# A decoder layer with a mixture of experts: attention scores in single PSUM banks, up to four row groups per step, and a planner that shares places and paces its preparations

## The chip, the core and the metric

The kernel runs on one core of one Trainium2 chip. The metric is the device time of one execution in microseconds (us); times of several executions are given by their median.

## The reference

One decoder layer over 32 sequences of 128 tokens, D = 128 features, 16 heads of 8 features. In short:

```python
def attn(q_in, kv_in, w, causal):          # B=32, S=128, H=16, HD=8
    Q, K, V = (heads(a @ w_ + b_) for ...)  # (B, S, H, HD)
    s = einsum('bqhd,bkhd->bhqk', Q, K) / sqrt(8)
    if causal: s = where(tril, s, -inf)
    return einsum('bhqk,bkhd->bqhd', softmax(s), V).reshape(B, S, D) @ w.wo + w.bo

x = layernorm(x + attn(x, x, sa, causal=True))        # self-attention
x = layernorm(x + attn(x, ctx_1024, ca, causal=False)) # cross-attention
p = softmax(x @ router_w + router_b)                   # E = 8 experts
topw, topi = top_k(p, 2); topw = softmax(topw)
# each token: sum over its 2 experts of
#   topw * (gelu(x @ w1[e] + b1[e]) @ w2[e] + b2[e]),  FF = 512, exact gelu
x = layernorm(x + moe)
```

All inputs and the output are float32. The 4096 tokens go to two experts each, so 8192 rows of 128 features pass through the experts' layers.

## The kernel before

**A planner orders the work.** The class Timetable (L80 to L195) holds every step of the kernel as a Task: an engine, a planned duration, a function that emits the instructions, the tasks it depends on, a priority, and the buffers that it takes from rings or uses. Timetable.run plays the steps through: an engine takes, whenever it is free, the ready task of the best priority whose buffers are free, and the instructions are emitted in that order. A step that depends on another engine's may start HOP = 0.35 us after it. The planned durations are constants in the code; they set only the order, and the chip's own times can differ. Engines are PE (TensorE), DVE (VectorE), ACT (ScalarE), POOL (GpSimd) and SP (which only issues transfers here).

**PE's rule.** On PE, a step that is not a score step goes first. A score step may be paired with a "mate" of the other kind and the other half h of the heads; the function emit_scores (L198) then emits the instructions of both in turn, lane by lane.

**Attention.** pair_item (L516 to L862) handles a pair of sequences p, once for self-attention ("s") and once for cross-attention ("c"): 16 pairs, 32 items. Its steps: load of x or of the context by SP (L536); transposes (PE L547, copied out by ACT); projections to Q and K (PE L590 and L591; ACT L595 and L600 copy them into tile qk); projection to V (PE L614, copied by DVE L618 into one of three v tiles); masking by heads on POOL (L631): from qk it makes kb and qb, in which each 32-row group holds four heads, with one head's rows kept for each 128 columns.

The scores are computed twice. by_query (L651) has queries on partitions, into tile bq: for each of two row groups of 32 rows, a product of 32 x 128 with 32 x 512 in float32 and, for self-attention, four causal masks of 32 x 512 in bfloat16 (L659), which add a large negative number. DVE takes the maximum over the keys (L675, 128 x 1024 in one instruction), splits it into three bfloat16 parts (L688 to L691), PE transposes them (L697) and DVE copies them (L702). by_key (L716) has keys on partitions, into tile bk, again two row groups of 512 columns; then "less" (L723) subtracts the queries' maxima by products in bfloat16, and the causal masks are added (L731). ACT takes exp (L746, 128 x 1024) into a pr tile, and PE multiplies with v (L760). Each item has two sequences and two halves h of the heads, so four by_query and four by_key steps. Tiles bq and bk are two PSUM banks each, and there is one of each; four further banks m0 to m3 take all other PE results.

Then: uT copy on ACT (L773), transposes back (PE L781), division by the sums on DVE (L789 and L790), transposes again, output projection (PE L807), addition of the residual (DVE L812), layer norm (normalize, L864: statistics on DVE L872 and L874, the reciprocal root on POOL L880 and L881, the rest on DVE L818 or L832). After cross-attention the normed rows lie twice in xrow, each with a number that tells where its result goes (L841); POOL makes x2 for the residual (L850 and L853); and route (L897 to L1022, once for each pair) computes the router's logits, the two best experts, their weights, and each row's place in its expert's region, and POOL scatters the rows to a DRAM tensor rowsD with one indirect transfer per 128 rows (L1010).

**Start.** PE first runs 14 products on zeros (pidle). ACT's queue carries, in this order, the loads of the attention's weights (L261 to L270), the filling of rowsD with empty rows (L463 and L468: ten transfers of 1548 KB, one of 1032 KB, two of 64.5 KB), the packing of the experts' weights into a DRAM tensor wpack (L469, L471, L476), and the load of b1 (L474). PE's first transpose after pidle is that of b1, pb (L481), and its result goes on into wpack (L484). sa.constant and ca.constant (L426 to L432) fold bv and wo into bo.

**Experts.** PHASES splits the sequences into the first 24 and the last 8. table(f) (L1070) works out on DVE, from the counts of rows per expert, a list of blocks of 4, 2 or 1 times 128 rows of one expert each: for the first phase 5, 7 and 21 blocks, for the second 23 blocks of 128 rows, that is 78 times 128 rows. block() (L1144): SP reads the block's expert and first row into registers and fetches rows (tile xg) and the expert's packed weights (tile wt, 578 KB) (L1153 to L1167); PE transposes (L1174), DVE copies (L1180), PE multiplies with w1 (L1194), ACT takes gelu (L1207), PE multiplies with w2 (L1222), DVE adds b2 (L1232), POOL scatters the result rows to DRAM tensor resD (L1239). The first transposes of a block wait in the plan for the last exp of the attention. Rings: xg 4, wt 4, xgT 2, h 2, y 3. final() (L1251): SP loads both results of each token (fyl, L1264), DVE adds them with their weights (L1277, L1280), layer norm, POOL L1296 and L1297, store by SP (L1302); ring yl of 3.

Of the kernel before, what the change touches and what calls it, by code (L numbers as in the profile page):

```python
# [9 lines left out]
F32 = mybir.dt.float32  # L10
# [13 lines left out]
S2 = 2  # L24
RG = 4
# [6 lines left out]
WROW = 2 * FF + NC + P  # L32
NOWHERE = 1 << 20
# [46 lines left out]
class Timetable:  # L80
# [3 lines left out]
    HOP = 0.35  # L84

    def __init__(self):
        self.tasks = []
        self.rings = {}
        self.tile = {}

    def ring(self, name, bufs):
        self.rings[name] = list(bufs)

# [5 lines left out]
    def run(self):  # L99
# [16 lines left out]
        def can(t):  # L116
            need = {}
            for r, k in t.acq:
                if k not in held:
                    need[r] = need.get(r, 0) + 1  # L120
            return all(len(self.rings[r]) >= n for r, n in need.items())

        def start(t, now, dur):
            for r, k in t.acq:
                if k not in held:
                    held[k] = (r, self.rings[r].pop(0))
                    self.tile[k] = held[k][1]
            waiting[t.eng].remove(t)
            t.end = now + dur
            heapq.heappush(ending, (t.end + t.lat, t.n, t))  # L130
            heapq.heappush(events, (t.end, -1))

        def finish(t, now):
            for a in t.after:
# [6 lines left out]
            for k in {*t.uses, *(k for _, k in t.acq)}:  # L141
                users[k] -= 1
                if not users[k]:
                    r, b = held.pop(k)
                    self.rings[r].append(b)

        while events:
# [5 lines left out]
            for e in waiting:  # L153
                while free[e] <= now + 1e-9:
# [4 lines left out]
                    pick = ok[0]  # L159
                    mate = None  # L160
                    if e == "PE" and any(t.kind for t in ok):
                        for t in ok:
                            if t.kind is None:
                                pick = t
                                break
                            mate = next(
                                (
                                    m for m in ok
                                    if m.kind and m.kind[0] != t.kind[0] and m.kind[1] != t.kind[1]
                                ),  # L170
                                None,
                            )
                            if mate:
                                pick = t
                                break
                        else:
                            pick = ok[0]
                    if mate is None:
                        start(pick, now, pick.dur)
                        pick.emit(self.tile) if not pick.kind else emit_scores([pick.emit], self.tile)  # L180
                        free[e] = now + pick.dur
                    else:
                        dur = max(pick.dur, mate.dur)
                        start(pick, now, dur)
                        start(mate, now, dur)
                        emit_scores([pick.emit, mate.emit], self.tile)
                        free[e] = now + dur
# [3 lines left out]
        if done != len(self.tasks):  # L191
            for e, w in waiting.items():
                print(e, [(t.n, t.acq, t.kind) for t in w][:20])
            print({k: v[1] for k, v in held.items()})
            raise AssertionError  # L195


def emit_scores(parts, tiles):  # L198

    lanes = [lane for part in parts for lane in part(tiles)]  # L200
# [7 lines left out]
def kernel(  # L208
# [37 lines left out]
    assert sum(n for n, _ in PHASES) == B  # L246
# [5 lines left out]


    idle = const.tile([P, 512], BF16, name="idle")
    nc.vector.memset(idle, 0.0)
    pidle = psum.tile([P, 512], F32, tag="m0", name="pidle")
    for _ in range(14):
        nc.tensor.matmul(pidle, lhsT=idle[:, :P], rhs=idle, start=True, stop=True)


    def load(src, shape, name, eng=nc.scalar):  # L261
        t = const.tile(shape, F32, name=name)
        eng.dma_start(out=t, in_=src)
        return t

    def column(src, name):
        return load(src.rearrange("(p o) -> p o", o=1), [P, 1], name)

    def row(src, n, name):
        return load(src.rearrange("(o n) -> o n", o=1).broadcast_to([P, n]), [P, n], name)  # L270

    T = Timetable()
    DUR = dict(xin=3, xT=3, qk=3, kb=5, qb=6, v=3, pr=5, t3=4, nmT=3, uT=2, o=2, oT=2, xn=3, xr=3,
               xrow=4, x2T=2)
    SHAPE = dict(
        xin=([P, S2, P], F32), xT=([P, S2, P], F32), qk=([P, 2, S2, P], F32),
        kb=([P, 4, P], F32), qb=([P, 4, P], F32), pr=([P, 8, P], F32),
        nmT=([P, P], BF16), uT=([P, S2, 2, P], F32), o=([P, S2, P], F32), oT=([P, S2, P], F32),
        xn=([P, S2, P], F32), xr=([P, S2, P], F32), xrow=([P, S2, 2, ROW], F32),
        x2T=([P, S2, P], F32),  # L280
    )
    for name, n in DUR.items():
        T.ring(name, [f"{name}{i}" for i in range(n)])
    T.ring("bq", ["bq"])
    T.ring("bk", ["bk"])
    T.ring("open", ["open0", "open1"])
    T.ring("m", ["m0", "m1", "m2", "m3"])
    NF = 6
    SMALL = ("nm", "ri", "st", "mv", "rs", "rt")
    for name in SMALL:  # L290
        T.ring(name, [f"{name}{i}" for i in range(NF)])

    def tl(key, shape=None, dtype=F32, name=None):

        tag = T.tile[key]
        base = tag.rstrip("0123456789")
        if shape is None:
            shape, dtype = SHAPE[base]
        T.tile[key] = work.tile(shape, dtype, tag=tag, name=name or f"{key[0]}_{'_'.join(map(str, key[1:]))}")
# [15 lines left out]
    def bank(key, shape, dtype=F32):  # L315

        tag = T.tile[key]
        n = 1024 if tag in ("bq", "bk") else 512
        flat = psum.tile([P, n], F32, tag=tag, name=f"{key[0]}_{'_'.join(map(str, key[1:]))}")
# [3 lines left out]

    ident = const.tile([P, P], F32, name="ident")
    make_identity(nc, ident)
    ident16 = const.tile([P, P], BF16, name="ident16")
    nc.vector.tensor_copy(ident16, ident)


    id32f = const.tile([P, RG, 32], F32, name="id32f")  # L330
    nc.vector.tensor_copy(id32f, ident.rearrange("p (g i) -> p g i", g=RG))
    id32 = const.tile([P, 32], BF16, name="id32")
    with nc.allow_low_precision("sums of zeros and a one"):
        nc.vector.tensor_reduce(id32, id32f.rearrange("p g i -> p i g"), AX.X, ALU.add)

    cauq = const.tile([P, 4, P], BF16, name="cauq")
    cauk = const.tile([P, 4, P], BF16, name="cauk")
    for t, s in ((cauq, 1), (cauk, -1)):  # L340
        nc.gpsimd.memset(t, 0.0)
        for g in range(RG):
            r = t[32 * g : 32 * g + 32]
            nc.gpsimd.affine_select(
# [1021 lines left out]
```

## Time and profile before

| | |
|---|---|
| three executions | 1180.70, 1196.39, 1190.12 us; median 1190.12 |
| the profiled execution: time | 1188.61 us |
| its span (first to last instruction) | 1186.8 us |
| mean granted TensorE clock in it | 0.712 of full |
| busy: PE, DVE, POOL, ACT | 950.9, 508.4, 409.8, 297.3 us |
| PE busy, 93 to 893 us (attention) | 749.7 of 800 us |
| PE busy, 893 to 1047 us (experts, first phase) | 121.6 of 154 us |
| first transpose of x; end of the last exp | 89.0 us; 887.4 us |

How to read the views. The page's slices cut the span into 40 equal parts of 29.7 us; a digit is the busy share in tenths, PEclk the granted clock in tenths, DMA the mean share of the 16 DMA engines. The table by stage gives for each engine the busy time and the number of instructions, then the granted clock, the DMA share and GB/s. A timeline line has start, duration, engine, line, operation, destination and sources, the tile on the array (rows*columns), and the size of the moving operand; instructions that belong together are put on one line with a count, and what an engine waited for stands in brackets. In the view of waits, an engine's line is followed by what it waited for, the total in us, the number of waits and the longest. PE's records give streaming time from a model of its pipeline, so the distance from one start to the next is the safer measure of a step.

### The profile page before, as it was taken

What the parts mean: (1) busy time and instruction counts of PE and PEld (TensorE: products, weight loads), DVE (VectorE), ACT (ScalarE), POOL (GpSimd) and SP (SyncE); (2) the same over time, 40 slices, a digit from 0 to 9 for tenths busy, and PEclk for the clock granted to TensorE, in tenths of its full rate; (3) what the DMA queues carried; (4) which work ended last, traced back from release to release, by engine and by line L of the source; (5) the groups of instructions that cost most, each with busy time, mean ns of one, the idle gap of its engine ahead of it and who ended that gap; (6) DMA issues with size and microseconds to landing.
All of it is one profiled execution on the core that took longest, in us unless ns stands there. A gap on an engine that the chain in (4) does not pass through costs nothing.

```text
span 1186.8 us, 18925 instructions
## 1 busy us (share of the span) xinstructions
PE 950.9 (80%) x7155; PEld 529.2 (45%) x7155; DVE 508.4 (43%) x1591; ACT 297.3 (25%) x578; POOL 409.8 (35%) x528
## 2 busy tenths in 40 slices
PE   1008999989999999899998898899998876665660
PEld 0004344545445454344544443444445765654560
DVE  2003235366543455645357647445556111136413
ACT  0002122323212242222333222223234333321120
POOL 3004013344322234432344522323335632236523
PEclk6556557668655677666798759566679999876695
DMA  6970000000000000000000000400001465666651
GB/s 218 376 186 14 1 5 14 6 19 10 15 4 19 8 10 19 10 9 13 12 10 19 14 8 3 139 1 1 10 10 56 143 188 180 203 199 189 183 162 53
DMA packets 61084, 81.30 MB, mean 69 GB/s; under 512 B 8702, under 2 KB 42531, under 8 KB 60993
## 3 DMA queue, kind: packets, MB, share of 16 engines
q1 hardware_dynamic: 36352, 48.79, 13.7%
q10 hardware_dynamic: 20096, 22.86, 6.2%
q0 software_dynamic: 4544, 8.44, 2.0%
q8 instruction: 57, 0.93, 0.3%
q14 instruction: 35, 0.28, 0.1%
HBM read 52.48 MB, written 33.21 MB: 72 GB/s over the span
## 4 chain that ended last, share of the span: by engine, by line
PE 57%; DVE 14%; issue 11%; POOL 6%; ACTq 5%; DMA 5%; ACT 1%; POOLq 0%; SPq 0%; DVEq 0%
PE bq_s L651 8%; PE bk_s L716 8%; PE bk_c L716 7%; PE bq_c L651 5%; PE po_c L760 4%; POOL res L1239 4%; PE po_s L760 4%; ACTq L463 3%; PE bq_s L659 3%; PE bk_s L731 2%; DVE nm_c L675 2%; ACTq L471 2%; PE bk_s L723 2%; PE bk_c L723 2%; DMA out_dram<-fxn 2%
## 5 line engine op out<-in xcount | busy, mean ns | idle before, releaser
L675 DVE TENSOR_REDUCE nm_s<-bq_s 128x8 f32<-128x1024 f32 x64 | 78.3, 1224 | 146.8 <-PE bq_s L659 146.8
L1194 PE MATMUL ph<-xgT,wt 128*128 128x128 f32 (+2 forms) x448 | 96.7, 368 | 40.4 <-DVE xgT L1180 26.3
L1239 POOL DMA_INDIRECT res<-y,xg x78 | 77.0, 987 | 135.3 <-DVE y L1232 123.1
L1207 ACT ACTIVATE h<-ph,wt 128x128 f32<-128x128 f32 (+2 forms) x224 | 75.4, 411 | 184.7 <-PE ph L1194 128.5
L1222 PE MATMUL po<-wt,h 128*128 128x128 f32 x624 | 91.6, 301 | 31.3 <-ACT h L1207 31.3
L746 ACT ACTIVATE pr_s<-bk_s 128x1024 f32<-128x1024 f32 x64 | 65.5, 1024 | 197.2 <-PE bk_s L731 191.7
L651 PE MATMUL bq_s<-kb_s,qk_s 32*128 32x512 f32 x256 | 107.3, 926 | 6.6 <-DVE nm_c L675 3.9
L746 ACT ACTIVATE pr_c<-bk_c 128x1024 f32<-128x1024 f32 x64 | 65.6, 1024 | 186.1 <-PE bk_c L723 186.1
L1010 POOL DMA_INDIRECT rows<-xrow_c,rt_c x64 | 64.2, 1003 | 137.0 <-DVE ri_s L789 38.2
L723 PEld LDWEIGHTS <-less 32*128 32x128 bf16 x1024 | 54.7, 122 | 118.0 <-issue 118.0
L716 PE MATMUL bk_c<-qb_c,qk_c 32*128 32x512 f32 x256 | 104.2, 902 | 3.1 <-ACT pr_c L746 3.0
L716 PE MATMUL bk_s<-qb_s,qk_s 32*128 32x512 f32 x256 | 105.4, 911 | 0.4 <-ACT pr_s L746 0.3
L1222 PEld LDWEIGHTS po<-wt,h 128*128 128x128 f32 x624 | 83.8, 211 | 39.3 <-ACT h L1207 38.4
L675 DVE TENSOR_REDUCE nm_c<-bq_c 128x8 f32<-128x1024 f32 x64 | 78.2, 1221 | 53.8 <-PE bq_c L651 53.8
L1194 PEld LDWEIGHTS ph<-xgT,wt 128*128 128x128 f32 x448 | 71.7, 230 | 57.1 <-DVE xgT L1180 36.6
L651 PE MATMUL bq_c<-kb_c,qk_c 32*128 32x512 f32 x256 | 88.1, 769 | 7.4 <-DVE nm_c L675 7.4
L631 POOL TENSOR_TENSOR kb_c<-qk_c,hmask 128x512 f32<-128x512 f32 x32 | 32.9, 1045 | 171.9 <-ACT qk_c L595 171.9
L1232 DVE TENSOR_TENSOR y<-po,wt 128x128 f32<-128x128 f32 (+2 forms) x56 | 19.2, 342 | 130.6 <-PE po L1222 124.8
L481 PE MATMUL pb<-ident,b 32*128 32x32 f32 x1 | 0.3, 281 | 80.3 <-DMA b<-in_L_xattn_e_b_dram 80.3
L581 POOL TENSOR_TENSOR xin_s<-xin_s,bos 128x256 f32<-128x256 f32 x16 | 11.6, 726 | 135.9 <-PE pxT_s L547 135.9
L760 PE MATMUL po_c<-pr_c,v 128*32 128x128 f32 x1024 | 56.6, 357 | 0.0
L760 PE MATMUL po_s<-pr_s,v 128*32 128x128 f32 x1024 | 54.1, 349 | 0.0
(225 smaller groups left out, 1424.4 us busy)
## 6 DMA issues: line engine op xcount, KB each, us to landing
wt<-wpack SPq DMA_DIRECT2D x56, 578.0 KB, 4.3
rows<-zrow ACTq DMA_DIRECT2D x10, 1548.0 KB, 16.0
fyl<-res SPq DMA_DIRECT2D x16, 256.0 KB, 3.9
xg<-rows SPq DMA_DIRECT2D x44, 64.5 KB, 2.9
xin_s<-in_x_dram SPq DMA_DIRECT2D x16, 128.0 KB, 2.1
xin_c<-in_ctx_dram SPq DMA_DIRECT2D x16, 128.0 KB, 2.2
wpack<-in_L_xattn_e_w_dram ACTq DMA_DIRECT2D x1, 2048.0 KB
wpack<-in_L_xattn_e_w_dram ACTq DMA_DIRECT2D x4, 512.0 KB
```

The source lines that it names most:

```text
L463: nc.scalar.dma_start(out=rows[at : at + m].rearrange("(n p b) d -> p n (b d)", p=P, b=4), in_=bc(zrow.rearrange("p b d -> p (b d)"), 1, m ...
L651: lambda d=d, i=i, rows=rows: nc.tensor.matmul(d[:, i], lhsT=t[qk][rows, 0, s, :], rhs=t[K("kb", s)][rows], start=True, stop=cross,)
L675: nc.vector.tensor_reduce(t[nm][:, 8 * h : 8 * h + 8], t[bq].rearrange("p i r k -> p (i r) k"), AX.X, ALU.max,)
L716: lambda d=d, i=i, rows=rows: nc.tensor.matmul(d[:, i], lhsT=t[qk][rows, 1, s, :], rhs=t[K("qb", s)][rows], start=True, stop=False,)
L723: lambda d=d, i=i, r=r, rows=rows: nc.tensor.matmul(d[:, i, r], lhsT=less[rows, r, :], rhs=t[nmT][rows, :], start=False, stop=cross and r ...
L746: nc.scalar.activation(tl(pr), t[bk].rearrange("p i r q -> p (i r) q"), AF.Exp, scale=SCALE)
L760: nc.tensor.matmul(d[32 * c : 32 * c + 32, s, h, :], lhsT=t[v][:, n, 32 * m : 32 * m + 32], rhs=t[pr][:, 2 * c + m, :], start=m == 0, stop ...
L1010: ins = nc.gpsimd.indirect_dma_start(out=rowsD[f][:, :], out_offset=bass.IndirectOffsetOnAxis(ap=r.idx[:, 2 * s + k : 2 * s + k + 1].bitca ...
L1194: nc.tensor.matmul(d[:, i, :], lhsT=t[wt][:, c * P : c * P + P], rhs=t[xgT][:, 0:size, :].rearrange("p b d -> p (b d)"), start=True, stop= ...
L1207: nc.scalar.activation(t[h][:, c, 0 : size * P], t[ph][:, i, :], AF.Gelu, bias=t[wt][:, 2 * FF + c : 2 * FF + c + 1],)
L1222: nc.tensor.matmul(d[:, b, :], lhsT=t[h][:, c, b * P : b * P + P], rhs=t[wt][:, FF + c * P : FF + c * P + P], start=c == 0, stop=c == NC - 1,)
L1239: ins = nc.gpsimd.indirect_dma_start(out=resD[f][:, :], out_offset=bass.IndirectOffsetOnAxis(ap=t[xg][:, b, P : P + 1].bitcast(U32), axis= ...
```

## The change

The changed kernel computes the same function. In words:

- **Scores.** A score step now covers one row group g and half of its four heads (u: 256 columns), into one PSUM bank that holds the row group's four heads; a bank takes two steps, u = 0 and then 1. The maximum (128 x 512, 256 of them) and exp (128 x 512, 256) follow bank by bank. The splitting of the maxima, their transposes and copies are done once per item for both sequences.
- **PE's rule.** choose() collects up to four ready score steps of different row groups, first at most two of a kind; it emits them when there are four, or three and nothing else is ready; otherwise other steps go first, and with nothing else it waits up to PATIENCE = 0.5 us of the plan before it emits fewer.
- **PSUM.** All eight banks are one ring; at most six hold scores.
- **SBUF.** Fourteen kinds of tiles share places: kb, qb, qk, xrow, uT, xg, xgT, h, y and yl take from 37 places "two", pr and wt from nine "big" (12 kinds), and the score banks bq and bk from the PSUM ring. Each kind keeps a limit; once the last score step has ended in the plan, the limits of the experts' kinds rise: xg 5 + 6, xgT 2 + 2, h 4 + 6 (h now by quarters of FF for a block of four), y 3 + 4, yl 2 + 2, wt 4 + 5.
- **Start.** The loads of the weights are issued by SP (four by ACT, one by POOL) in the order of their first use; b1 is 25th on SP. The filling of rowsD becomes 32 transfers of 516 KB and the packing of the weights one task per expert and part; all are SP tasks in the planner, at planned times behind the loads of x, and the transpose of b1 and the bias constants are PE tasks there. Row scatters depend on the fills of their phase, fetches of blocks on the packing. v's zeros, the counting masks and the table's constants are made on POOL, the causal masks on DVE.
- **Other engines.** The copy of v moves from DVE to ACT (L752), xrow's second copy to ACT (L957), the addition of epsilon from POOL to DVE (L993); route works on four sequences at a time; running counts are kept on POOL (L1090).
- **Experts.** A phase's blocks of different sizes are interleaved; a block's fetch skips the check of its registers' bounds; final's loads and stores are issued by ACT (L1386, L1413) rather than SP.
- **Plan.** HOP is 0.3, and most planned durations are set anew.

(Line numbers in this list are those of the changed kernel.) The diff, cut to its core:

```diff
-    HOP = 0.35
+    HOP = 0.3
+    LANES = 3
+    PATIENCE = 0.5
...
+    def share(self, name, n, of, more=0):
+        self.rings[name] = [name] * n
+        self.back[name] = of
+        self.more[name] = more
...
+        def choose(ok, now):
+            lanes, other = [], next((t for t in ok if t.kind is None), None)
+            for most in (2, RG):
+                for t in ok:
+                    if (
+                        t.kind
+                        and all(m.kind[1] != t.kind[1] for m in lanes)
+                        and sum(m.kind[0] == t.kind[0] for m in lanes) < most
+                        and can(t, *lanes)
+                    ):
+                        lanes.append(t)
+            if len(lanes) == RG or not other and len(lanes) >= self.LANES:
+                return lanes
+            if other:
+                return [other]
+            if now - idle["PE"] >= self.PATIENCE:
+                return lanes
+            return None
...
         def finish(t, now):
+            if t.kind:
+                scores[0] -= 1
+                if not scores[0]:
+                    for r, n in self.more.items():
+                        self.rings[r] += [r] * n
...
 def emit_scores(parts, tiles):
-    lanes = [lane for part in parts for lane in part(tiles)]
+    lanes = [part(tiles) for part in parts]
...
-    T.ring("bq", ["bq"])
-    T.ring("bk", ["bk"])
-    T.ring("m", ["m0", "m1", "m2", "m3"])
+    SHARES = dict(
+        kb=("two", 5, 0), qb=("two", 6, 0), qk=("two", 4, 0), xrow=("two", 5, 0), uT=("two", 2, 0),
+        xg=("two", 5, 6), xgT=("two", 2, 2), h=("two", 4, 6), y=("two", 3, 4), yl=("two", 2, 2),
+        pr=("big", 5, 0), wt=("big", 4, 5), sc=("m", 6, 0),
+    )
+    T.ring("m", [f"m{i}" for i in range(8)])
...
-    step = 6 * FILL
-            nc.scalar.dma_start(
-                out=rows[at : at + m].rearrange("(n p b) d -> p n (b d)", p=P, b=4), ...
-    nc.scalar.dma_start(out=wpack[:, :, 0:FF], in_=e_w1)
-    b1 = load(e_b1.rearrange("e (c f) -> (e c) f", f=P), [E * NC, P], "b1")
-    nc.tensor.transpose(pb, b1, ident[: E * NC, : E * NC])
+            at, step = 0, 2 * FILL
+                def fill(t, f=f, at=at, m=m):
+                    nc.sync.dma_start(
+                        out=rowsD[f][at : at + m].rearrange("(n p b) d -> p n (b d)", p=P, b=4), ...
+                piece(f, fill, 2.2, 150.0 + 800 * f)
+            def w12(t, e=e):
+                nc.sync.dma_start(out=wpack[e, :, 0:FF], in_=e_w1[e])
+                nc.sync.dma_start(out=wpack[e, :, FF : 2 * FF]..., in_=e_w2[e]...)
+            pack(e, w12, 5.0)
+        a = T.add("PE", 0.1, tb, (), 500.0, [("m", pb)])
...
-                    for i in range(2):
-                        g = 2 * h + i
-                            lambda d=d, i=i, rows=rows: nc.tensor.matmul(
-                                d[:, i], lhsT=t[qk][rows, 0, s, :], rhs=t[K("kb", s)][rows],
+            for g in range(RG):
+                for u in range(2):
+                    def by_query(t, s=s, u=u, bq=bq, rows=rows):
+                        two = slice(2 * u, 2 * u + 2)
+                            lambda: nc.tensor.matmul(
+                                d[:, two], lhsT=t[qk][rows, 0, s, :], rhs=t[K("kb", s)][rows, two],
...
-                    nc.vector.tensor_reduce(
-                        t[nm][:, 8 * h : 8 * h + 8], t[bq].rearrange("p i r k -> p (i r) k"),
-                        AX.X, ALU.max,
-                    )
+                    nc.vector.tensor_reduce(t[nm][:, s, 4 * g : 4 * g + 4], t[bq], AX.X, ALU.max)
...
-                        tl(pr), t[bk].rearrange("p i r q -> p (i r) q"), AF.Exp, scale=SCALE
+                            t[pr][:, 4 * i : 4 * i + 4, :], t[bk], AF.Exp, scale=SCALE
...
-            nc.vector.tensor_copy(
+            nc.scalar.copy(
                 t[v].rearrange("p n (h c) -> p n h c", h=2)[:, :, :, 0:HD],
...
-            ins = nc.sync.dma_start(
-                out=tl(yl, [P, S2, 2, P])...
+            ins = nc.scalar.dma_start(
+                out=tl(yl)...
...
-            for _ in range(m):
-                block(f, k, size, tb, a1, last_scatter[f], 1e5 * (f + 1) + 10 * k)
+            for i in range(m):
+                todo.append(((i + 0.5) / m, k, size))
+        for i, (_, k, size) in enumerate(sorted(todo)):
+            block(f, k, size, tb, a1, 1e5 * (f + 1) + 10 * i)
```

## The prediction

> **What bounds the kernel now.** I read the slices first, then busy time by stage, then single PE steps, then the DMA queue's waits. Slices:
>
> ```profile
> PE   1008999989999999899998898899998876665660
> ...
> PEclk6556557668655677666798759566679999876695
> DMA  6970000000000000000000000400001465666651
> ```
>
> For three slices (89 us) PE does nothing and DMA is full: ACT's queue writes the empty rows, and b1, which PE's first transpose needs, is queued behind them. Attention follows, PE at 9 but PEclk about 6. From slice 30 on come the experts, with DMA at 5 to 6 and PE at 6 to 8. The same by stages (PE, PEld, DVE, ACT, POOL busy, then clock):
>
> ```profile
> 0.00:93.00 93.00, 10.49 (x33) 6.25 (x34) 9.16 (x31) 2.96 (x6) 11.95 (x37) 0.56 0.82 252
> 93.00:893.00 800.00, 749.69 (x5970) 361.53 (x5969) 402.64 (x1219) 218.64 (x346) 271.51 (x337) 0.69 0.05 15
> 893.00:1047.00 154.00, 121.57 (x773) 100.79 (x771) 38.69 (x137) 49.49 (x136) 63.08 (x67) 0.93 0.51 159
> ...
> 1161.00:1187.00 26.00, 0.00 (x0) 0.00 (x0) 11.11 (x41) 0.00 (x0) 10.51 (x17) 0.50 0.20 61
> ```
>
> In attention PE is busy 750 of 800 us, the next engine 403: PE is the bound, at a granted clock of 0.69. The clock is only ever 0.5 or 1.0, so 38% of that time is at full. What a step costs at half clock:
>
> ```profile
> 326.44 2.08 PE L716 MATMUL bk_s<-qb_s,qk_s 32*128 32x512 f32 x4
> 328.31 0.63 PE L723 MATMUL bk_s<-nmT_s,less 32*128 32x128 bf16 x8
> 328.88 0.62 PE L731 MATMUL bk_s<-cauk,id 32*32 32x512 bf16 x8
> 329.43 2.08 PE L651 MATMUL bq_s<-kb_s,qk_s 32*128 32x512 f32 x4
> 331.44 0.62 PE L659 MATMUL bq_s<-cauq,id 32*32 32x512 bf16 x8
> ```
>
> and a step of four row groups at full clock:
>
> ```profile
> 638.36 0.70 PE L651 MATMUL bq_c<-kb_c,qk_c 32*128 32x512 f32 x2 [0.66 <-DVE nm_c L675]
> 638.37 0.70 PE L716 MATMUL bk_c<-qb_c,qk_c 32*128 32x512 f32 x2
> ...
> 639.34 0.39 PE L723 MATMUL bk_c<-nmT_c,less 32*128 32x128 bf16 x8
> ```
>
> Start to next start: two groups 1.87 to 2.01 us at half clock (1.06 at 635.91, full clock); four groups 0.98 at full. So groups run side by side, and two more are free. In the last stage SP waits to refill its four xg tiles until old results have landed:
>
> ```profile
> SPq L1160 <- DMA res<-y,xg: 222.8, 29, 138.3
> ```
>
> **The change part by part.** I sum against the profiled execution's own 1188.6 us (span 1186.8 and 1.8 around it; the median of the runs is 1190.1). Stages: A to PE's first x transpose at 89.0, B to the last exp's end at 887.4 (798), C the rest (299).
>
> *A, loads and fills.* b1 becomes the 25th transfer on SP; issues there start 0.50 us apart, so it goes out at 13.3 and lands 2.0 to 3.9 us later (like the other small loads). From b1's landing to the first x transpose took 2.7 us. First transpose at about 19: 70 us less (60 if POOL's constants, now with the zeroing of v at 1.1 us each, are late; 75 at best). The same 17 MB of fills and the weight copies, 16 x 0.5 MB of them in a row, now run beside attention, where DMA is 5% busy; at the 376 GB/s of slice 2 such a row takes 22 us, and an x load queued behind it is covered by the ring of four x tiles (a pair of pairs, 40 us of PE work). Without that cover PE waits 22 us once. First row scatters come some 80 us in, after the 34 us of their fills.
>
> *B, PE.* A 128x256 f32 product streams in 0.432 us, so 512 columns take 0.85 (1.71 at half clock); a step adds 0.11 (0.16), and each change of tile shape, scores or less to masks and back, another 0.10 (0.14). Less is 0.05 per row, a mask round of 256 columns 0.11, twice that at half clock. Before, in issue order: 204 two-group steps and 26 of four; with their less and masks 315 us at full clock, 592 at half. After, the built order has 1024 half-size products in 327 runs, mostly of three or four groups: 94 runs alternate less and masks (1.26 to 1.35 us at full clock), 97 have each once (0.95), 63 less only (0.74), 57 masks only (0.84), 16 neither: 320 at full, 576 at half. The rest of PE's work, products with v (128 x 0.574 or 1.012), projections and transposes, is the same 220 or 410. **Sum: 534 (full) or 1002 (half) before, 540 or 985 after.** More groups side by side is thus paid back by steps of half the columns and twice the switches; what can move is the clock. Check on before: 38% of the time at full gives 1/(0.38/534+0.62/1002) = 752, measured 746.
>
> What sets the clock: I took each 3.41 us stretch of the clock record and added streaming time at full clock times the share of the array that an instruction covers. All 146 stretches followed by full clock have 1.23 us or more, all 205 followed by half have 1.30 or less: the gate is 36% of the array. Two-group steps give 39 to 42% at full clock, so a tenth of waiting drops it, and 21% at half, so only a burst (products with v, 42%) lifts it. After: four-group steps give 60 to 69% at full and 33 to 37% at half, three-group 42 to 51%; alternating three-group ones 33%. The average over all PE work is equal (58% and 32%), so it is the spread and the waits that decide.
>
> Waits: one bq tile forces reduce, 1.22 us, between two query steps; six one-bank tiles let several steps run ahead. DVE: 256 reduces of 512 elements, between 0.61 (half) and 1.22; 128x16 takes 0.17, so by length 0.69: 177 for 157, +20; four max-splitting operations on 32 tiles for 64, -38; routing per four sequences -30; v copies go to ACT -14. ACT: 256 exps at about 0.60 (a 512-wide copy takes 0.58) for 131, +23; v +13, second row copy +6. POOL loses 8 us of adds to DVE and gains as much. DVE 340, ACT 261, POOL 272 in B, all under 540, so none ends the stage; eight shared banks, of which open outputs hold one or two, may still make PE wait. Bounds for the full-clock share: 0 and 1. I take 0.6, above today's 0.38 because the steps clear the gate by more, and no more because a fifth of the steps do not: 1/(0.6/540+0.4/985) = 659, plus 45 of PE idle (50 now) = 704. **B: -94.**
>
> The Trainium skill's "TensorE: Matmul & The Clock Gate", section "HAM oscillation", blames clock drops on idle gaps of more than about 3.4 us. Here the clock is 0.50 from 110 to 175 us with PE busy 65.00 of 65.00. By the rule attention would be at full clock before and after, and B would give almost nothing. The Trainium skill's "TensorEngine Tiling (Array Packing)", section "Key Properties", says that a change of tiling mode drains the engine. That speaks against this change, and the rows price it at 0.10 to 0.14 us.
>
> *C, experts.* 78 row blocks at full clock: 0.11 (transpose) + 0.89 + 0.95 = 1.95 us, 152 in all; 6 until it runs; 26 of tail (1161 to 1187) stay. Floor 184. Deeper xg (11), wt (9) and h, mixed block sizes, and result loads and stores on ACT's queue take the 223 us wait away; behind a late result load gelus now wait, one landing (3.2 us) each. Next late is DMA: 49 MB at today's 190 GB/s would be 258, +32 = 290; slices of 326 GB/s occur, giving 150, beside PE. I keep half of PE's present waits for h and xgT (57), 33: 217, since the peak rate is nearest to deep prefetch. **C: -82** (-9 to -115).
>
> Reordering by the planner's new costs issues nothing new; its effect is counted in the built order above. Sum: 1188.6 - 70 - 94 - 82 = **943**.
>
> **Rivals.** (1) *The clock share stays 0.38*: 750+45 = 795, B -3, total 1034. For it: equal work and unloaded average; against: a deeper ring. (2) *Full clock nearly throughout* (0.95): 553+45 = 598, B -200, total 837. For it: walked without waits, four fifths of the steps clear the gate; against: alternating steps. (3) *Locked at half clock*, in attention, the slower side: PE 985+45 = 1030, B +232, total 1269. It decides if the share falls below 0.07, where B passes 974; if C gains only 9, below about 0.2. For it: 32% average at half clock is under the gate, and evener mixing has fewer bursts; against: today's half-clock spells end, and four-group steps reach 37% even there. (4) *DMA holds the experts at today's rate*: C -9, total 1016; for it 62% DMA at 190 GB/s, against it the 326.
>
> **How the numbers follow.** Forecast (share 0.5 to 0.75, C -60 to -105): 0.52, own range 875 to 1003. Rival 1: 0.20. Rival 2: 0.12. Rival 3: 0.07. Rival 4: 0.06, and 0.03 for what I don't see, taken as no change. Range 830 to 1070 leaves out rival 3 and the unseen. Faster by over 2% (about what a measurement tells from no change): 0.52+0.20+0.12+0.06 = 0.90; same 0.03; slower 0.07.
>
> **What would show it.** First x transpose near 19 us; PE still the busiest engine in attention, with a busy time near 540/share; clock in B about 0.8; one score run near 0.54 to 0.64 us at full clock, alternating runs 1.3; SP's wait for results gone, experts near 217 us. Wrong if records in mask groups of 16 start much wider apart than today's 3 ns (issue then bounds PE), if DVE or bank waits leave PE under 85% busy, or if x loads are late behind fills.

## The result, and the profile after

| | before | after |
|---|---|---|
| median | 1186.46 us (4 runs, 1180.7 to 1196.39) | 911.32 us (4 runs, 909.42 to 913.32) |
| ratio | | 0.767 (95% interval 0.762 to 0.773) |
| profiled execution, span | 1188.61, 1186.8 us | 911.36, 909.6 us |
| A, to the first transpose of x | 89.0 us | 17.9 us |
| B, to the end of the last exp | 798.4 us | 692.4 us |
| C, the rest of the span | 299.4 us | 199.3 us |
| full-clock share of B | 0.376 | 0.567 |

Ratios here and below leave out disturbed executions of either kernel, so they can differ a little from the quotient of two medians; the traces of experiments 6, 11 and 12 are of such executions, each the slowest of its four.

A clock that is only ever 0.5 or 1.0 gives the full-clock share: twice the mean granted clock, less one.

The slices of the changed kernel's page, the rows that answer to those of before:

```profile
PE   5997999999999969999999999999955999999830
...
PEclk7776978559969978558699996957785899999975
DMA  5761524300000010000000010013010768869941
```

PE starts in the first slice, and DMA is busy beside it for the first seven slices and not ahead of it. PEclk still swings, between 5 and 9, but lies higher. From slice 31 to 36 the experts run with PE at 9. In the view of SP's waits, the 222.8 us for results ahead of the row fetches are gone but for 1.0. What is left of waits for free tiles is for the weights' places, and for the last results at the end:

```profile
SPq L1292 <- DVE y L1354: 50.8, 16, 7.2
...
SPq L1470 <- DMA res<-y,xg: 16.5, 1, 16.5
```

The stages, in the table by stage (PE, PEld, DVE, ACT, POOL busy, then clock, DMA share, GB/s):

```profile
0.00:17.90 17.90, 7.71 (x20) 3.23 (x21) 6.36 (x16) 1.28 (x1) 12.43 (x45) 0.79 0.48 113
17.90:710.30 692.40, 655.34 (x7984) 399.18 (x7982) 322.32 (x989) 243.18 (x506) 271.98 (x356) 0.78 0.16 50
710.30:860.00 149.70, 145.00 (x1096) 131.28 (x1097) 60.48 (x206) 70.81 (x211) 87.15 (x97) 0.98 0.80 260
```

The whole of C, before and after:

```profile
887.40:1186.80 299.40, 196.28 (x1193) 164.87 (x1192) 99.91 (x355) 79.25 (x233) 126.33 (x155) 0.82 0.51 154
710.30:909.60 199.30, 155.78 (x1185) 141.40 (x1185) 100.16 (x346) 76.52 (x231) 123.95 (x144) 0.89 0.70 225
```

In attention PE is busy 655 of 692 us and the next engine 399 (weight loads, beside PE) and 322: PE is still the bound, at a clock of 0.78 for 0.69. A run of three and one of four groups in self-attention at half clock, on the timeline:

```profile
37.96 1.23 PE L852 MATMUL bk_s<-qb_s,qk_s 32*128 32x256 f32 x6
38.98 0.43 PE L857 MATMUL bk_s<-nmT_s,less 32*128 32x128 bf16 x6
39.34 0.42 PE L768 MATMUL bk_s<-cauk,id 32*32 32x256 bf16 x12
39.69 1.24 PE L852 MATMUL bk_s<-qb_s,qk_s 32*128 32x256 f32 x8
40.70 0.44 PE L857 MATMUL bk_s<-nmT_s,less 32*128 32x128 bf16 x8
41.07 0.44 PE L768 MATMUL bk_s<-cauk,id 32*32 32x256 bf16 x16
```

The fourth group costs 0.02 us: start to next start 1.73 us for three groups, 1.75 (to 41.44) for four. And a run of three groups at full clock that alternates less and masks:

```profile
208.98 0.48 PE L793 MATMUL bq_c<-kb_c,qk_c 32*128 32x256 f32 x1
208.99 0.48 PE L852 MATMUL bk_s<-qb_s,qk_s 32*128 32x256 f32 x1
209.00 0.48 PE L793 MATMUL bq_s<-kb_s,qk_s 32*128 32x256 f32 x1
...
209.53 0.21 PE L857 MATMUL bk_s<-nmT_s,less 32*128 32x128 bf16 x1
209.67 0.28 PE L768 MATMUL bq_s<-cauq,id 32*32 32x256 bf16 x1
209.88 0.22 PE L857 MATMUL bk_s<-nmT_s,less 32*128 32x128 bf16 x1
210.03 0.28 PE L768 MATMUL bq_s<-cauq,id 32*32 32x256 bf16 x1
```

The next run starts at 210.26: 1.28 us, of which 0.73 lie behind the scores, in four small rounds.

### The profile page after: what moved, and what is told of

It reads as the page before. It is cut to its first block, busy times and chain, and to the rows that moved or that the text cites. A ratio compares the mean times of both kernels' runs of the same rounds, so it can differ in the third digit from the quotient of the medians.

```text
span 909.6 us, 22744 instructions
## 1 busy us (share of the span) xinstructions
PE 818.8 (90%) x9187; PEld 543.8 (60%) x9187; DVE 428.8 (47%) x1351; ACT 321.0 (35%) x738; POOL 408.4 (45%) x543
## 4 chain that ended last, share of the span: by engine, by line
PE 79%; DVE 8%; POOL 4%; DMA 3%; issue 3%; SPq 1%; ACT 1%; POOLq 0%; ACTq 0%; DVEq 0%
PE bk_c L852 11%; PE bq_s L768 7%; PE bk_s L852 7%; PE bq_c L793 6%; PE po_c L887 5%; PE po L1344 5%; PE ph L1319 5%; PE po_s L887 5%; PE bq_s L793 4%; PE bk_s L768 3%; PE bk_c L857 3%; PE bk_s L857 2%; PE pqk_c L720 2%; PE pqk_s L720 2%; DVE fxn L1400 2%
## 5 line engine op out<-in xcount | busy, mean ns | idle before, releaser
L808 DVE TENSOR_REDUCE nm_s<-bq_s 128x4 f32<-128x512 f32 x128 | 83.7, 684 | 117.8 <-PE bq_s L768 99.3
L793 PE MATMUL bq_s<-kb_s,qk_s 32*128 32x256 f32 x512 | 130.5, 502 | 0.9 <-ACT pr_s L873 0.7
L873 ACT ACTIVATE pr_c<-bk_c 128x512 f32<-128x512 f32 x128 | 71.7, 597 | 146.9 <-PE bk_c L857 146.8
L808 DVE TENSOR_REDUCE nm_c<-bq_c 128x4 f32<-128x512 f32 x128 | 82.9, 684 | 79.0 <-PE bq_c L793 78.7
L873 ACT ACTIVATE pr_s<-bk_s 128x512 f32<-128x512 f32 x128 | 73.4, 598 | 131.7 <-PE bk_s L768 131.5
L852 PE MATMUL bk_c<-qb_c,qk_c 32*128 32x256 f32 x512 | 117.0, 568 | 0.0
L852 PE MATMUL bk_s<-qb_s,qk_s 32*128 32x256 f32 x512 | 112.5, 515 | 0.2 <-ACT pr_s L873 0.2
L793 PE MATMUL bq_c<-kb_c,qk_c 32*128 32x256 f32 x512 | 93.6, 454 | 1.7 <-POOL kb_c L777 1.7
L1124 POOL DMA_INDIRECT rows<-xrow_c,rt x64 | 63.1, 986 | 59.4 <-DVE rt L1142 18.5
L768 PE MATMUL bq_s<-cauq,id 32*32 32x256 bf16 x1024 | 82.9, 306 | 0.0
```

The lines of the kernel that those rows point to most:

```text
L768: lambda j=j: nc.tensor.matmul(d[32 * j : 32 * j + 32, two], lhsT=id32[rows], rhs=bc(causal[rows, j, :], 1, 2), start=False, stop=True,)
L793: lambda: nc.tensor.matmul(d[:, two], lhsT=t[qk][rows, 0, s, :], rhs=t[K("kb", s)][rows, two], start=True, stop=cross,)
L808: nc.vector.tensor_reduce(t[nm][:, s, 4 * g : 4 * g + 4], t[bq], AX.X, ALU.max)
L852: lambda: nc.tensor.matmul(d[:, two], lhsT=t[qk][rows, 1, s, :], rhs=t[K("qb", s)][rows, two], start=True, stop=False,)
L873: nc.scalar.activation(t[pr][:, 4 * i : 4 * i + 4, :], t[bk], AF.Exp, scale=SCALE)
L1124: ins = nc.gpsimd.indirect_dma_start(out=rowsD[f][:, :], out_offset=bass.IndirectOffsetOnAxis(ap=r.idx[:, 2 * s + k : 2 * s + k + 1].bitca ...
```

## The experiments

Ratios are to the kernel before on the same chip, with 95% intervals. Runs one to four came from one chip, five to eight from a second, nine to twelve from a third. On the second chip the experts took 228 to 230 us in kernels whose experts are the changed kernel's (199 to 204 on the others), so those runs are compared by stages and with each other. The step prices named below are those of the prediction.

### 1. b1 early, in the kernel before

```diff
+    b1 = load(e_b1.rearrange("e (c f) -> (e c) f", f=P), [E * NC, P], "b1", nc.sync)  # behind the first x
     sa = Attn(sa_wq, ...)
...
-    b1 = load(e_b1.rearrange("e (c f) -> (e c) f", f=P), [E * NC, P], "b1")           # behind the fills
```

> The kernel before, with one line moved: b1 is loaded on SP's queue right behind the first x, no longer on ACT's queue behind the fills. If the 89 us ahead of the first x transpose were only the wait for b1, the first transpose comes near 19 us, the fills run beside attention, and the time falls by 60 to 75 us (to about 1115 to 1125). Rival: the fills take the DMA engines from the x loads or ACT's queue from its copies, the wait only moves to a later place, and the gain is under 30 us.

Measured: median 1169.19 us, ratio 1.000 (0.989 to 1.011), which counts two executions of the kernel before on this chip, 1163.62 and 1169.59 us. The first transpose does come at 17.7 us, and then nothing of x's chain follows. In the view of waits, ACT's copy of the transposed x:

```profile
ACT L559 <- DMA wpack<-in_L_xattn_e_b_dram: 88.7, 1, 88.7
```

ACT issues fills and packs one after the other until 88.6 us (eight of the fills take 23.09 us to issue), and its first copy, at 89.95 us, is behind them. In the kernel before it was at 89.67. The rival holds: two things ended the 89 us together, b1's place in the queue and ACT's own issuing, and taking one away gives nothing that the interval can tell.

### 2. 64 rows per score product, in the kernel before

```diff
-   d[:, i], lhsT=t[qk][rows, 0, s, :], rhs=t[K("kb", s)][rows],
+   d[:, i], lhsT=t[qk][64*i : 64*i+64, 0, s, :], rhs=t[K("kb", s)][64*i : 64*i+64],   # by_key likewise
```

> The kernel before, with every score product contracted over 64 rows in place of 32 (the scores are then sums over two heads, so this is for its time alone). The same instructions and the same columns stream, only the share of the array that a product covers doubles; the 26 steps of four groups now need two passes, at most 26 x 0.85 = 22 us more at full clock. If the clock follows the covered share of the array, two-group steps now give over 70% at full clock, the clock in attention goes from 0.69 to over 0.9, PE's 748 us there to 560 to 620, and the time falls to 980 to 1050. Rival: the clock follows how long PE is busy or idle, not what it covers; then it stays at 0.69 and the time is 1190 to 1220.

Measured: 1028.12 us, ratio 0.881 (0.875 to 0.887). Attention in the table by stage:

```profile
89.40:724.60 635.20, 585.65 (x5944) 280.94 (x5943) 401.86 (x1209) 215.04 (x345) 271.09 (x336) 0.96 0.06 19
```

The same instructions, DVE, ACT and POOL as before (401, 217, 273), and PE 586 us in place of 748, at a clock of 0.96. Nothing was made shorter; the products only cover twice as much of the array. The share of full clock is 0.912.

### 3. 16 rows per score product, in the changed kernel

```diff
-   d[:, two], lhsT=t[qk][rows, 0, s, :], rhs=t[K("kb", s)][rows, two],
+   d[:, two], lhsT=t[qk][rows.start : rows.start+16, 0, s, :],
+                  rhs=t[K("kb", s)][rows.start : rows.start+16, two],                 # by_key likewise
```

> The changed kernel, with every score product contracted over 16 rows in place of 32 (half of each group's heads are left out of the scores, so this is for its time alone). Instructions, columns and waits stay. If the clock follows the covered share of the array, runs of four groups fall from 60 to 69% to about 35% at full clock, just under the gate of 36%; the share of full clock in attention falls from 0.56 to 0.15 to 0.35, and the time rises by 120 to 230 us, to 1030 to 1140. Rival: what counts is the tile of 32 rows that a product takes, or how long PE is busy: 911, within 10.

Measured: 1082.61 us, ratio 0.927 (0.917 to 0.937), against 0.767 for the changed kernel.

```profile
17.80:868.40 850.60, 815.55 (x7985) 476.83 (x7983) 321.47 (x989) 245.61 (x506) 271.79 (x356) 0.60 0.13 41
```

PE takes 816 us where it took 655 for the same columns; the share of full clock is 0.197. DVE, ACT and POOL are within 3 us of the changed kernel's. With the second experiment this settles that the covered rows, and not PE's busy time, set the clock here. Both edits also change the data, since half or twice the heads enter a product; but data is not needed to raise the clock: the 14 products on zeros at the start, 128 x 128 from 1.25 to 7.33 us in the changed kernel's trace, are followed by full clock at 7.13 us.

### 4. Less for all lanes, then masks, in the changed kernel

```diff
 def by_query(...):
-       ] + masks(d, two, cauq, rows)
+       ] + [None, None] + masks(d, two, cauq, rows)
 def emit_scores(parts, tiles):
-            if k < len(lane):
+            if k < len(lane) and lane[k]:
```

> The changed kernel, with the lanes of a run emitted in phases: scores, then less, then masks (query lanes skip two places), so that the 94 runs that alternate less and masks have each once. From the same step prices PE's sum in attention falls from 540 to 508 at full clock and from 985 to 934 at half clock; at today's share of full clock, 0.56, that is 40 us; the low-covered rounds grow shorter, so the share may rise to 0.7, another 45. Expected 825 to 875. Rival: alternating costs nothing beside the DVE, ACT and bank waits: 900 to 915.

Measured: 833.8 us, ratio 0.715 (0.711 to 0.719), 77 us below the changed kernel's median (7% by the ratios, 0.715 and 0.767). B is 611.7 us with PE busy 575 and a share of 0.703. One mixed run of three lanes, at full clock, from 34.47 to the next at 35.46, 0.99 us:

```profile
34.47 0.48 PE L852 MATMUL bk_s<-qb_s,qk_s 32*128 32x256 f32 x2
34.49 0.48 PE L793 MATMUL bq_s<-kb_s,qk_s 32*128 32x256 f32 x1
...
35.01 0.28 PE L857 MATMUL bk_s<-nmT_s,less 32*128 32x128 bf16 x4
35.22 0.28 PE L768 MATMUL bk_s<-cauk,id 32*32 32x256 bf16 x2
35.22 0.28 PE L768 MATMUL bq_s<-cauq,id 32*32 32x256 bf16 x1
```

Against 1.28 for the alternating run above. Both halves of the expectation show: shorter runs, and more time at full clock.

### 5 and 6. Whole banks, alone and with the phases

```diff
-                for u in range(2):            # 256 columns each
+                for u in range(1):            # two = slice(0, 4): 512 columns, four less, masks of 512; planned durations to match
```

> The changed kernel, with a score step covering a row group's whole bank (512 columns, four less and four masks of 512) in place of two halves of 256. The built order has 178 runs for 327; from the same step prices PE's sum in attention falls from 540 to 514 at full clock and from 985 to 958 at half, 28 us at today's share. But rounds that alternate less and masks are longer, and walked without waits the order holds full clock for 0.85 of the time, not 0.91: a share of 0.50 would eat the gain. Expected 880 to 930. Rival: halves are what lets PE's plan fill four lanes; then waits grow and it is over 950.

> The changed kernel with both edits: whole banks, and scores, less and masks in phases. The step prices give 465 at full clock and 875 at half; walked without waits the order holds full clock for 0.98. With a share of 0.65 to 0.85 and 37 us of idle PE, attention takes 535 to 595 us where it takes 692, and the time is 755 to 815, below the 834 of phases alone. Rival: with fewer PE steps another engine ends the stage (DVE 322 and ACT 243 of 692 us now), or banks held twice as long leave PE waiting: 820 to 850.

Measured: 920.71 us, ratio 0.768 (0.757 to 0.779), for whole banks alone; 863.63 us, 0.717 (0.706 to 0.729), with phases. Alone, B is 670.6 us at a share of 0.590, as the step prices give: 1/(0.59/514 + 0.41/958) = 635 us, PE busy 636. With phases the expectation failed: B is 630.2 us where 535 to 595 was expected. PE's prices held (1/(0.58/465 + 0.42/875) = 579, measured 586) and PE waited 45 us; what failed is the share, 0.58 for the expected 0.65 or more. The rows overstate the miss: the trace is of 877.96 us, while the other three executions took 852.17 to 864.71, and the experts take 228.4 us here for 199.3, which the expected 755 to 815 did not hold; with these 29 us it is 784 to 844. Neither rival (another engine, bank waits) shows. Why longer steps held less full clock than the halves of experiment 4 (0.703), and how much of that is this one execution, was not isolated.

### 7. At most two lanes, in the changed kernel

```diff
-    LANES = 3
+    LANES = 2
...
+                        and len(lanes) < 2
-            if len(lanes) == RG or not other and ...
+            if len(lanes) == 2 or not other and ...
```

> The changed kernel, with at most two row groups per step (the lanes of choose cut to 2), all else as it is. The step prices give 670 at full clock and 1252 at half (540 and 985 with four); two-group runs cover 39 to 42% at full clock and 21% at half, so the share falls back to about the 0.38 of the kernel before: 942 us plus 37 idle in attention, a time near 1200 (1080 if the share stays at 0.6). Rival: the gain in attention came from the ring of banks, the merged small steps and the other engines, not from four groups: under 1000.

Measured: 1068.23 us, ratio 0.891 (0.876 to 0.906). The share came as expected, 0.367, but PE was busy 771.7 us in B and not 942. Worked back from that share, and from half clock costing 1.85 times full clock, PE's sum is 547 at full clock and 1013 at half. Without the share, from the steps in the traces timed start to next start, each kind at either clock, it is about 538 and 984, and 534 and 941 in the changed kernel. My 670 and 1252 charged the fixed 0.11 us to each half of a bank and not once to a run. So with two lanes the sum is nearly that of four, and it is the clock that makes B 825 us in place of 692.

### 8. Short rings for the experts, in the changed kernel

```diff
-        xg=("two", 5, 6), xgT=("two", 2, 2), h=("two", 4, 6), y=("two", 3, 4), yl=("two", 2, 2),
-        pr=("big", 5, 0), wt=("big", 4, 5), sc=("m", 6, 0),
+        xg=("two", 5, 0), xgT=("two", 2, 0), h=("two", 4, 0), y=("two", 3, 0), yl=("two", 2, 0),
+        pr=("big", 5, 0), wt=("big", 4, 0), sc=("m", 6, 0),
```

> The changed kernel, with the limits of the experts' kinds not raised after the last score step (xg 5, wt 4, xgT 2, h 4, y 3, yl 2 throughout). If depth is what took the experts from 299 to 199 us, that stage grows by 30 to 80, to a time of 940 to 990. Rival: the order of block sizes, the result loads on ACT's queue, and packed weights that wait no longer for the fills did it: 905 to 925.

Measured: median 1009.11 us of two runs (996.26 and 1021.95), with no interval. C is 256.4 us against 228 to 230 in runs five to seven: depth is worth 27 us there, just under the 30 expected. SP again waits 30.1 us for results ahead of the row fetches, and PE's waits in C come back, near the 26.3 and 31.3 us of the kernel before:

```profile
PE ph L1319 <- DVE xgT L1305: 25.1, 21, 5.4
PE po L1344 <- ACT h L1332: 20.0, 21, 4.4
```

B, which the edit does not touch (PE's order is the same up to the last score step but for a few neighbours), took 720.5 us at a share of 0.540; the total is thus no measure of the rings.

### 9. Paced pieces on SP, in the kernel before

```diff
+    def sp(out_, in_, us, prio, to):
+        to.append(T.add("SP", us, lambda t: nc.sync.dma_start(out=out_, in_=in_), (), prio, lat=3.0))
...
-            nc.scalar.dma_start(out=rows[at : at + m]...)       # and the packs; b1 early as in 1
+            sp(rows[at : at + m]..., 2.2, 150.0 + 800 * f, filled[f])
...
-        l0 = add("SP", 0.1, ld, acq=[("xin", xin)], lat=3.0)
+        l0 = add("SP", 0.5, ld, acq=[("xin", xin)], lat=3.0, prio=-100.0)
...
-                    add("POOL", 1.2, sc, [i, dd], ...)
+                    add("POOL", 1.2, sc, [i, dd, *filled[f]], ...)
```

> The kernel before, with b1 loaded early as in the first experiment, and with the fills and the packing of the weights as paced tasks on SP in the planner, in the pieces of the changed kernel. Now neither b1 nor ACT's own queue holds the start: the first copy of a transposed x on ACT, at 90 us with b1 moved alone, comes near 20 us. If that is the whole of the first stage's gain, and the transfers beside attention cost nothing, the time falls by 60 to 75 us against the kernel before, the rest of the trace as it was. Rival: x loads late behind the pieces give back 20 us or more; under 45 us gained.

Measured: 1107.34 us, ratio 0.956 (0.952 to 0.959). The ratio counts executions of the kernel before of 1154.23 to 1160.77 us on this chip, so the gain is some 51 us, between the expected 60 to 75 and the rival's 45. In the trace the first stage does give its 71 us: ACT's first copy starts at 18.36 us, the first transpose at 17.7. B is 792.4 us and C 297.2, close to the trace of the kernel before (798.4 and 299.4), but that trace is not of the executions counted here: its span, 1186.8 us, is longer than they are. So some 20 of the 71 us were lost behind the first stage, and no run shows where. PE waits 61 us in B for 50; these 11 us may be the price of the transfers beside attention, which was not isolated.

### 10. Fills and packs at once, in the changed kernel

```diff
-                piece(f, fill, 2.2, 150.0 + 800 * f)
+                piece(f, fill, 2.2, -250.0 + f)
...
-            ws.append(T.add("SP", us, fn, (), 600.0, lat=3.0))
+            ws.append(T.add("SP", us, fn, (), -240.0, lat=3.0))
```

> The changed kernel, with all fills and packing pieces issued on SP ahead of the loads of x from the fourth on (no pacing). Some 25 MB at 300 GB/s are 80 us; the fourth tile of x or context, wanted by PE at about 60 us, lands near 100. If pacing is what keeps PE fed, PE waits 25 to 45 us there, and the time is 930 to 960. Rival: the transfers share the DMA engines in any order and the x loads land in time: 905 to 920.

Measured: 894.54 us, ratio 0.775 (0.770 to 0.780); the interval meets that of the changed kernel, and the expected 930 to 960 failed. The fourth tile is issued at 86.1 us, nearly as late as expected, and PE is busy 79 of the 102 us from 18 to 120, against 96 in the changed kernel:

```profile
18.00:60.00 42.00, 31.81 (x334) 19.29 (x336) 8.83 (x24) 8.94 (x19) 9.94 (x13) 0.58 1.06 376
60.00:120.00 60.00, 47.30 (x512) 29.09 (x507) 20.34 (x49) 13.23 (x28) 14.06 (x17) 0.61 0.51 104
```

That loss of 17 us was there, and was paid back: PE's order came out otherwise (527 at full clock for 540) and the share of full clock was 0.661. In the total, pacing is worth nothing that was measured.

### 11. Waiting for four lanes, with the phases

```diff
-    LANES = 3
-    PATIENCE = 0.5
+    LANES = 4
+    PATIENCE = 1.5
```

> The phases of the fourth experiment, and the planner holds out for four lanes: LANES 4 for 3, PATIENCE 1.5 us for 0.5. The built order has 256 score runs for 327, 235 of them of four groups; the step prices give 438 us at full clock and 808 at half (508 and 934 with phases alone). The work is 39% of the array even at half clock, above the gate of 36%: only waits can then keep the clock down. With a share of 0.7 to 0.95 and 50 to 90 us of waits, attention takes 510 to 590 us for 612, and the time is 735 to 810. Rival: a run must wait for its slowest lane, PE idles over 130 us, the clock drops in the waits, and the time is 820 or more.

Measured: 794.68 us, ratio 0.681 (0.672 to 0.691): the best of all, below the changed kernel by 11% (ratios) or 13% (medians).

```profile
17.70:593.10 575.40, 529.00 (x7982) 341.40 (x7980) 339.57 (x987) 237.07 (x504) 263.17 (x344) 0.87 0.20 60
```

PE is busy 529 us at a clock of 0.87 and waits 46. The waits stayed small; the share is 0.743. At that share the step prices give 1/(0.743/438 + 0.257/808) = 496, so they fall 6% short here; timed from the trace as in experiment 7, the sums are about 474 and 804, so it is the price at full clock that was too low.

### 12. Order of blocks and queue of the results as before, in the changed kernel

```diff
-                todo.append(((i + 0.5) / m, k, size))
+                todo.append((k, k, size))
...
-            ins = nc.scalar.dma_start(        # results; the output's store likewise
+            ins = nc.sync.dma_start(
```

> The changed kernel, with the blocks of a phase in the order of before (sizes 4, 2, 1 one after the other) and the results loaded and the output stored by SP; the deep rings stay. The experts fell from 299 to 199 us, and short rings gave back 27 of these 100 (256 against 228 to 230 in the three other kernels of that call). If the order of sizes and ACT's queue for the results are the rest, the stage grows by 40 to 70 us, to a time of 950 to 980. Rival: the rest came with the lanes of SBUF in attention's end and cheaper fetches, and deep rings absorb either order: 205 to 215, a time of 915 to 930.

Measured: 917.98 us, ratio 0.774 (0.762 to 0.786). C is 204.8 us: the rival holds, these two edits alone gave at most 6 of the 100 us. B has PE's order of the changed kernel again and took 714.4 us at a share of 0.497.

## Why the prediction held, and where it was off

Forecast 943 us, measured 911.32, inside both the range and the likeliest case's own range. (The lower end of that own range, worked out again from share 0.75 and C -105, is 869 and not 875.)

- **A, -70.** Measured -71.1 (89.0 to 17.9). The size is right, and the stated cause is half of it. "b1, which PE's first transpose needs, is queued behind them" was true, but experiment 1 shows that this wait could go and nothing be gained, since ACT's queue held its first copy to the same microsecond. The change takes both away, as experiment 9 does.
- **B, -94.** Measured -106.0. The statement that PE's sums are equal at full clock and that "what can move is the clock" is what experiments 2, 3 and 7 and the timed sums (534 at full clock after, 535 before) show: with the columns unchanged the clock alone moves attention by -163 us (798.4 to 635.2) and by +158 (692.4 to 850.6), and with two lanes in place of four the sum stays within 3% and the share falls from 0.567 to 0.367. The share of 0.6 that I chose was 0.567. That was a choice between 0.38 and 0.95 and did not follow from the working: nearly equal sums gave 0.497 to 0.661 in experiments 8, 10 and 12, so that it came so close is in part luck. PE's busy time by my prices at that share is 1/(0.567/540 + 0.433/985) = 671, measured 655; idle 45 forecast, 37 measured.
- **The gate of 36%.** By the working of the prediction, stretches of the changed kernel that were followed by full clock have at least 1.24 us of covered time in 161 of 162 cases, those followed by half clock at most 1.25 in 106 of 107. The same boundary, 1.2 to 1.3 us, parts them in the other profiled experiments, with a few exceptions down to 1.07 and up to 1.34.
- **The Trainium skill's page "TensorE: Matmul & The Clock Gate", section "HAM oscillation",** puts the drops down to idle gaps of more than about 3.4 us. In B of the kernel before PE idles longer than that once (10.3 us), and the clock drops 16 times. In experiment 2 PE's idle time is 50 us of 635 and in experiment 3 it is 35 of 851; the kernel with less idle time has the lower clock (0.60 to 0.96). The measurement decides: on this case the rule does not tell what to do, and the covered share does.
- **Switches of tile shape.** The Trainium skill's page "TensorEngine Tiling (Array Packing)", section "Key Properties", says that a change of tiling mode drains the engine. No row shows the drain itself; that changes cost time shows in 1.28 us for an alternating run and 0.99 for a grouped one. I priced that in and left it there; experiment 4 shows that it was the cheapest thing to change: putting less ahead of masks takes 77 us off.
- **C, -82.** Measured -100.1. The mis-sized term is "half of PE's present waits for h and xgT (57), 33" (half of 57 is 29, so the sum itself should have been 939): next to nothing of them was left (PE is busy 145.0 of 149.7 us from 710 to 860), and DMA moved 260 GB/s, so that rival 4, with 190, was wrong. Of the 100 us depth accounts for 27 (experiment 8), order and queue for at most 6 (experiment 12). The remainder, some 70, is open: the larger limits that hold from the start, h by quarters, and a fetch without checks were not tried one by one. Nor were short rings tried together with the old order and queue; as with the two waits ahead of the first transpose, the two may cost more together than apart. What the rows of C do show is where the 100 us lie: 60 are PE's idle time (103 to 44 us) and 40 its busy time (196 to 156 us for nearly the same instructions, at a clock of 0.89 for 0.82). And SP's 222.8 us, which the prediction read as the last stage's, hold one wait of 138.3 that began in attention, near 773 us, and ended at 911; behind that 84.5 us remain.
- **Rivals 1 to 3** differ only in the clock's share, and the runs sit between: 0.567, from 0.38 (rival 1) to 0.95 (rival 2). Rival 3's locked clock is what experiment 3 comes near to, at 0.197.

## What to carry to other kernels

Where PE is the bound and its granted clock is below 1, count what its instructions cover of the array (rows times columns), and not only how long they run: packing side by side paid here through the clock, while the sum of steps stayed the same. Group instructions of one tile shape across lanes, and hold a step back until its lanes are full: those two edits, a few lines, took the changed kernel down by another 11% (ratios of 0.681 and 0.767). And when an engine starts late, look at every queue that the first step passes; one of two equal waits taken away gives nothing.

## What the runs showed of the hardware that was not expected

- The clock follows active rows, not the row group that a product occupies: 16 active rows of a group's 32 lowered the share of full clock from 0.567 to 0.197, and 64 rows in place of 32 in the kernel before raised it from 0.376 to 0.912. Products on zeros raise it too.
- One and the same order of PE instructions in attention took 692.4, 714.4 and 720.5 us in three profiled executions of kernels that differ only after it, at shares of 0.567, 0.497 and 0.540. Experiments 8 and 12 ran on different chips, PE's idle time was 37, 35 and 50 us, and which difference moved the share is not shown. Edits worth less than these 4% of the stage can't be judged from one trace.
- Issuing transfers holds the issuing engine: eight fills of 1548 KB took ACT 23.09 us to issue, 2.9 us each, where a small load took 0.33 to 0.49. The time does not go by bytes alone: four transfers of 512 KB in the packing behind the fills took 23.18 us, 5.8 each.
